# A four-layer graph network on one core: messages weighted by ScalarE, one-hots in halves, and a test by in-degree

## The chip, the cores and the metric

The kernel runs on one core of a Trainium2 chip. The metric is device time in microseconds (us). A profile of one execution gives, for each engine, when each instruction ran; the profiled execution has a time of its own, which stands beside the median of the runs below. Engine names are those of the profile: PE (TensorE), DVE (VectorE), ACT (ScalarE), POOL (GpSimd) and SP (SyncE, which here only starts DMAs).

## What is computed

The reference carries 3125 nodes with 256 features through four layers. Each layer adds a graph network and a token mixer to x, and then a mixture of experts. All four graph networks use the same 50,000 edges, drawn and sorted by destination like this:

```python
src = jax.random.randint(jax.random.fold_in(_gk, 2), (50000,), 0, 3125, jnp.int32)
dst = jnp.minimum((3125 * jax.random.uniform(jax.random.fold_in(_gk, 3), (50000,)) ** 2.0).astype(jnp.int32), 49999)
```

Layer 1's graph network (with two convolutions, each with an edge weight `ew`) and layer 3's (three convolutions, without weights) are, cut to what matters:

```python
def _hconv(x, src, dst, ew, w1, b1, w2, b2, g, b):            # layer 1, twice
    h = jax.nn.relu(x @ w1 + b1)
    msg = ew[:, None] * h[src]
    agg = jax.ops.segment_sum(msg, dst, num_segments=x.shape[0])
    h = agg @ w2 + b2
    return jax.nn.relu(_bn(h, g, b))

deg = jnp.zeros((n,), x.dtype).at[dst].add(1.0) + 1.0         # layer 3
dinv = jax.lax.rsqrt(deg)
h = jnp.tanh(gcn_conv(x, W1, b1, src, dst, dinv))             # 256 -> 512
h = jnp.tanh(gcn_conv(h, W2, b2, src, dst, dinv))             # 512 -> 512
out = gcn_conv(h, W3, b3, src, dst, dinv)                     # 512 -> 256
```

where `gcn_conv` is A·(h W) + b, with the adjacency A (self loops included) scaled by `dinv` on both sides.

## The kernel before

Nodes lie in NB = 25 blocks of P = 128. The edges of each block are padded to whole slots of 128; there are room and instructions for NS = 416 slots, which are handled in groups of G = 4, so a loop over the edges has 104 groups. Line numbers are those of the kernel before, as in its profile.

**A loop over the edges** is `gather_sum` (L550). For each group it issues four indirect DMAs from POOL (`gather`, L531), each of which fetches the source rows of one slot into the tile `msg`; it makes four one-hot matrices on DVE from the slot's local destinations `dl` (with weights: four `tensor_scalar` at L566, which compare with the column numbers `cols` and multiply by `ew`; without: one `tensor_tensor` over 128x512 in `one_hot`, L538); it adds the group before it into `agg` (L544, four adds on DVE, each at an address that L527 loads into a register); it lets PE multiply one-hots by messages (L585, called from `sum_group`), with four PSUM tiles named `g`; and it takes one step of the other work that was passed in as `steps`. The messages have `ahead` tiles of 128x1024, seven where nothing else is said. Afterwards the build orders the instructions of each engine, so neighbours on an engine need not be neighbours in the source.

**Layer 1** (L1681) has two such loops with weights, each 256 wide. In both, `both()` takes a step of the mixer `mix1` and a step of `more` per group. In the first loop `more` is `sorted_edges`, in the second it is `counts` (L2071). `counts` prepares layer 3: it writes a dense matrix of edge counts between all nodes, `counted`, to DRAM, in bfloat16. It goes over NR = 40 runs of edges. Per run it makes two one-hots of 128x3200 in bfloat16 on DVE (`ohs` and `ohd`, L2085, one buffer each); `on`, an identity or zero (L2089, ACT); for 25 blocks a 128x128 matmul (L2098) on top of `on` times the previous run's tile (L2096); copies of the sums into the tile `T` (L2100, ACT); an identity added to the own block of `T` where a run begins (L2108, DVE); two ACT passes over `T` (L2111) that write to `junk` and accumulate whatever lies over FULL = 255.5 into `over`; and the DMA of `T` to `counted` (L2112, SP). It yields twice per run, so 80 times, once per group in the first 80 of 104 groups.

At its end (L2114 to L2120) `over` is reduced to a column of `unfit`, which holds for three conditions whether a partition violates them; the columns are summed over partitions into one number, `gathers`.

**Layer 3** (L2325) reads that number into a register and takes one of two branches, both of which are in the program:

```python
with tc.If(unfit > 0, preferred_fallthrough_block=False) as cmp:
    with self.pool("xT", 1) as xp:
        self.xT = xp.tile([P, 2, NP], F32, name="xT")
        self.gcn3()
    self.routes(begin, route)
with cmp.Else():
    self.dense3(begin, route)
```

`dense3` (L2123) multiplies by `counted`: 100 products (four sets of 25 blocks), each a DMA of 800 KB into a tile `a` and 75 matmuls (L2154) with activations split into three bfloat16 parts; the scaling by `di` = 1/sqrt(deg + 1) is at L2160, the weight matmuls are at L465 and L2214, and the mixer's steps and `routes` (the assignment of tokens to experts, which ends with 50 indirect DMAs `sent<-xs` on POOL at L1402) run beside the products. `gcn3` (L2256) does the same with three unweighted loops over the edges, `gather_sum` with `ahead=6`: it normalizes x and stores a table of 256-wide rows; the first loop gathers from it, with the mixer's steps beside it; each of 25 blocks is scaled, transposed, multiplied by W1 and passed through tanh, and stored as a 512-wide row table; the second loop gathers 512-wide; groups of four blocks go through W2, tanh and W3 into a third table, 256 wide; the third loop gathers from it; the sum is scaled and added to x. Then come `routes`, with nothing beside them. The experts (`rest`) follow either branch.

`self.deg`, from which both branches take `di`, is made in layer 0: an extra column of the messages is set to one (L854), summed like the features, and copied out at L901. So it is the number of edges that end at each node.

Of the kernel before, what the change touches and what calls it, by code (L numbers as in the profile page):

```python
# [9 lines left out]
F32 = mybir.dt.float32  # L10
BF16 = mybir.dt.bfloat16
I32 = mybir.dt.int32
AF = mybir.ActivationFunctionType
# [6 lines left out]
P = 128  # L20
# [10 lines left out]
G = 4  # L31
# [33 lines left out]
class Net:  # L65
# [466 lines left out]
            out=out, out_offset=None, in_=table,  # L532
            in_offset=bass.IndirectOffsetOnAxis(ap=self.src[:, t:t + 1], axis=0))

    def one_hot(self, pool, g):

        oh = pool.tile([P, G, P], F32, name="oh")
        self.nc.vector.tensor_tensor(oh, bc(self.dl[:, g * G:(g + 1) * G], [None, None, P]),  # L538
                                     bc(self.cols, [None, G, None]), ALU.is_equal)
        return oh  # L540

    def add_to(self, agg, t, q, w):
# [4 lines left out]
        for j in range(G):  # L547
            self.add_to(agg, g * G + j, q[j], agg.shape[2])

    def gather_sum(self, pool, ps, table, w, agg, weighted=False, ahead=7, steps=None):  # L550

        nc = self.nc
        sums = {}
        n = 1024 // w
        for g in range(NS // G):
            msg = []
            for j in range(G):
                if j % n == 0:
                    m = pool.tile([P, n, w], F32, name="msg", bufs=ahead)
                self.gather(m[:, j % n, :], table, g * G + j)  # L560
                msg.append(m[:, j % n, :])
            if weighted:
                oh = pool.tile([P, G, P], F32, name="oh", bufs=3)
                for j in range(G):
                    t = g * G + j
                    nc.vector.tensor_scalar(oh[:, j, :], self.cols, self.dl[:, t:t + 1], self.ew[:, t:t + 1],  # L566
                                            op0=ALU.is_equal, op1=ALU.mult)
# [1113 lines left out]
    def layer1(self):  # L1681
        nc, tc = self.nc, self.tc
        self.norm_x()
        with self.pool("rooms", 1) as c, self.pool("gnn", 1) as gw, self.pool("gnn2", 2) as gp, \
                self.pool("mix", 1) as mw, self.pool("mix2", 2) as mp, \
                self.pool("ps1", 3, PSUM) as ps, ExitStack() as own:
            pool = Pools(gw, gp, CONV_ONE)

            sums = ps.tile([P, 3, P], F32, name="acc0", bufs=1)
            nc.scalar.copy(sums[:, 1, :], self.cols)  # L1690
            nc.vector.tensor_scalar(sums[:, 2, :], self.cols, 1.0, None, op0=ALU.add)
            steps = self.mix1(mw, mp, ps, sums[:, 0, :])

            def loop(tab, agg, more):
                def both():
                    for _ in range(NS // G):
                        next(steps, None)
                        next(more, None)
                        yield

                self.gather_sum(pool, ps, tab, D, agg, weighted=True, steps=both())
                for _ in more:
                    pass


            self.rooms = c.tile([P, NR, 2 * NB], BF16, name="rooms")
            self.run_blk = c.tile([1, NR], I32, name="run_blk")
            self.goes_on, self.begins = (c.tile([P, NR], F32, name=n) for n in ("goes_on", "begins"))

            self.unfit = c.tile([P, 3], F32, name="unfit")  # L1710

            tab, agg, *rest = self.conv_head(pool, ps, 1, self.xT)
            with self.pool("sort", 1, side="right") as bp:
                with ExitStack() as inner:
                    loop(tab, agg, self.sorted_edges(bp, ps, inner, sums[:, 1, :]))
            with self.pool("res", 1, side="right") as hp:
                hT = hp.tile([P, 2, NP], F32, name="hT")
                self.conv_tail(pool, ps, agg, *rest, hT)
                sc, sh = self.batch_norm(pool, hT, self.plain(gw, "L1_gnn_bn1_g"), self.plain(gw, "L1_gnn_bn1_b"), "bn")
                self.relu_of(hT, sc, sh)  # L1720
                tab, agg, *rest = self.conv_head(pool, ps, 2, hT)
            with self.pool("count", 1, side="right") as bp:
                loop(tab, agg, self.counts(bp, ps, sums[:, 1:, :]))
            hp = own.enter_context(self.pool("res", 1, side="right"))
            hT = hp.tile([P, 2, NP], F32, name="hT")
# [345 lines left out]
    def counts(self, p, ps, cols):  # L2071
# [1 line left out]
        nc = self.nc  # L2073
        ident = p.tile([P, P], BF16, name="identb")
        nc.vector.tensor_copy(ident, self.ident)
        full = p.tile([P, 1], F32, name="full")
        nc.vector.memset(full, -FULL)
        over = p.tile([P, NR, 2], F32, name="over")
        nc.vector.memset(over, 0.0)
        last = None  # L2080
        for u in range(NR):
            oh = []
            for k, name in enumerate(("ohs", "ohd")):
                t = p.tile([P, NB, P], BF16, name=name)
                nc.vector.tensor_tensor(t, bc(self.rooms[:, u, k * NB:(k + 1) * NB], [None, None, P]),  # L2085
                                        bc(cols[:, 1 - k, :], [None, NB, None]), ALU.is_equal)
                oh.append(t)
            on = p.tile([P, P], BF16, name="on", bufs=2)
            nc.scalar.mul(on, ident, self.goes_on[:, u:u + 1])  # L2089
            yield  # L2090
            T = p.tile([P, NB, P], BF16, name="T", bufs=2)
            for k0 in range(0, NB, 4):
                n = min(4, NB - k0)
                q = ps.tile([P, 512], F32, name="mm")[:, :n * P]
                if last is not None:
                    nc.tensor.matmul(q, on, last[:, k0:k0 + n, :], start=True, stop=False)  # L2096
                for k in range(n):
                    nc.tensor.matmul(q[:, k * P:(k + 1) * P], oh[0][:, k0 + k, :], oh[1][:, k0 + k, :],  # L2098
                                     start=last is None, stop=last is None or k == n - 1)
                nc.scalar.copy(T[:, k0:k0 + n, :], q.rearrange("p (k d) -> p k d", d=P))  # L2100
                if k0 == 12:
                    yield

            Tf = T.rearrange("p k d -> p (k d)")
            r = nc.values_load(self.run_blk[0:1, u:u + 1], engines=(ET.DVE, ET.SP), min_val=0, max_val=NB - 1,
                               skip_runtime_bounds_check_because=IN_RANGE)
            own = Tf[:, bass.ds(r * P, P)]
            nc.vector.scalar_tensor_tensor(own, ident, self.begins[:, u:u + 1], own, op0=ALU.mult, op1=ALU.add)  # L2108
            for i, k0, k1 in ((0, 0, 13), (1, 13, NB)):
                junk = p.tile([P, 13 * P], BF16, name="junk")[:, :(k1 - k0) * P]  # L2110
                nc.scalar.activation(junk, Tf[:, k0 * P:k1 * P], AF.Relu, bias=full, accum_out=over[:, u, i:i + 1])  # L2111
            nc.sync.dma_start(self.counted[bass.ds(r * P, P), :], Tf)  # L2112
            last = T
        nc.vector.tensor_reduce(self.unfit[:, 1:2], over.rearrange("p u i -> p (u i)"), axis=AX.X, op=ALU.max)  # L2114
        nc.vector.tensor_scalar(self.unfit[:, 1:2], self.unfit[:, 1:2], 0.0, None, op0=ALU.is_gt)
        one = p.tile([P, 1], F32, name="one")
        nc.vector.tensor_reduce(one, self.unfit, axis=AX.X, op=ALU.add)
        q = ps.tile([P, 512], F32, name="mm")
# [328 lines left out]
```

## Time and profile before

| | us |
|---|---|
| median of three runs | 6186.31 (6184.32 to 6188.53) |
| the profiled execution | 6189.69 |
| its span | 6187.9 (mean granted TensorE clock 0.862) |
| layer 1's first loop, first to last gather | 1500 to 2058 |
| layer 1's second loop, first gather to last add | 2166.1 to 2836.0 |
| layer 3's branch, `di` to the last `sent<-xs` | 4476.8 to 5696.8 |

Over the span PE is busy 75%, DVE 53%, POOL 39% and ACT 25%. These are averages over stages with different limits, so the stages are read one by one: windows of the trace give each engine's busy time and instructions ("x") in a stretch, with the granted clock, the DMA share and GB/s; tables by line give busy time, the mean duration of one instruction in ns, and what ended the idle time before it.

### The profile page before, as it was taken

What the parts mean: (1) busy time and instruction counts of PE and PEld (TensorE: products, weight loads), DVE (VectorE), ACT (ScalarE), POOL (GpSimd) and SP (SyncE); (2) the same over time, 40 slices, a digit from 0 to 9 for tenths busy, and PEclk for the clock granted to TensorE, in tenths of its full rate; (3) what the DMA queues carried; (4) which work ended last, traced back from release to release, by engine and by line L of the source; (5) the groups of instructions that cost most, each with busy time, mean ns of one, the idle gap of its engine ahead of it and who ended that gap; (6) DMA issues with size and microseconds to landing.
All of it is one profiled execution on the core that took longest, in us unless ns stands there. A gap on an engine that the chain in (4) does not pass through costs nothing.

```text
span 6187.9 us, 81932 instructions
## 1 busy us (share of the span) xinstructions
PE 4643.9 (75%) x25310; PEld 3283.6 (53%) x25310; DVE 3297.2 (53%) x8633; ACT 1567.8 (25%) x4108; POOL 2397.0 (39%) x2340
## 2 busy tenths in 40 slices
PE   1848775696778766656697758880699999997997
PEld 1314343583565344443683235550456888786996
DVE  6448777426798388876326567776142100134222
ACT  1213233222100245432222123311144201111332
POOL 1537774322777275552423567771100000011111
PEclk9969887797897777777798879995899999998998
DMA  2744442553333144332564324430111322124554
GB/s 82 220 122 117 118 120 66 179 177 102 93 97 102 55 151 137 130 117 66 160 184 131 99 72 123 120 116 27 57 62 65 131 99 73 59 96 153 182 172 160
DMA packets 385095, 710.60 MB, mean 115 GB/s; under 512 B 100817, under 2 KB 223256, under 8 KB 384652
## 3 DMA queue, kind: packets, MB, share of 16 engines
q1 hardware_dynamic: 266431, 425.79, 21.6%
q0 software_dynamic: 108064, 269.63, 14.9%
q10 hardware_dynamic: 10157, 9.80, 0.5%
q8 instruction: 213, 3.49, 0.2%
q14 instruction: 230, 1.88, 0.1%
HBM read 571.51 MB, written 133.47 MB: 114 GB/s over the span
## 4 chain that ended last, share of the span: by engine, by line
PE 43%; issue 17%; DVE 15%; POOL 11%; DMA 8%; ACT 3%; DVEq 2%; SPq 1%; ACTq 0%; another core or an unknown queue 0%; POOLq 0%
PE dn L2154 13%; PE mm L465 6%; POOL msg L531 6%; PE g L585 4%; PE g L862 3%; DMA msg<-L_gnn_htab,src 2%; PE h L1507 2%; PE y L1520 2%; DVE ohd L2085 2%; POOL ase L531 2%; DVE agg L544 2%; DMA terms<-outr 2%; POOL back L1524 1%; PE mm L2214 1%; PE mm L2098 1%
## 5 line engine op out<-in xcount | busy, mean ns | idle before, releaser
L531 POOL DMA_INDIRECT msg<-L_gnn_c_tab,src x832 | 827.4, 995 | 606.6 <-issue 225.3
L531 POOL DMA_INDIRECT msg<-L_gnn_htab,src x832 | 887.5, 1067 | 383.5 <-issue 213.0
L544 DVE TENSOR_TENSOR agg<-agg,g 128x256 f32 (+2 forms) x1664 | 697.6, 419 | 215.0 <-PE g L862 96.3
L2154 PEld LDWEIGHTS <-a 128*128 128x128 bf16 x7500 | 736.2, 98 | 116.9 <-issue 28.3
L862 PE MATMUL g<-msg,oh 128*128 128x261 f32 (+1 forms) x1664 | 568.7, 450 | 194.0 <-DVE agg L544 176.5
L1402 POOL DMA_INDIRECT sent<-xs,ids x150 | 153.0, 1020 | 1292.9 <-DMA yb<-done,backs 1036.3
L585 PE MATMUL g<-msg,oh 128*128 128x256 f32 x1664 | 581.6, 484 | 86.5 <-DMA msg<-L_gnn_c_tab,src 35.5
L862 PEld LDWEIGHTS g<-msg,oh 128*128 128x128 f32 x1664 | 314.2, 211 | 433.6 <-DVE agg L544 328.2
L585 PEld LDWEIGHTS g<-msg,oh 128*128 128x128 f32 x1664 | 358.5, 238 | 235.4 <-DVE oh L566 86.8
L1524 POOL DMA_INDIRECT back<-y,toi x168 | 163.6, 974 | 787.1 <-DVE y L1523 510.6
L1507 PE MATMUL h<-xe,w 128*128 128x128 f32 x3584 | 436.8, 278 | 5.3 <-DMA w<-in_L_ffn_W 5.2
L2154 PE MATMUL dn<-ha,a 128*128 128x256 bf16 x3750 | 428.5, 275 | 7.7 <-ACT ha L2139 6.5
L1520 PE MATMUL y<-w,hT 128*128 x1792 | 431.2, 388 | 0.0
L1511 ACT ACTIVATE hT<-h,br 128x128 f32<-128x128 f32 x896 | 256.4, 369 | 669.5 <-issue 573.4
L1507 PEld LDWEIGHTS h<-xe,w 128*128 128x128 f32 x3584 | 422.0, 195 | 7.0 <-DVE toi L1496 6.2
L2154 PE MATMUL dn<-hb,a 128*128 128x256 bf16 x3750 | 418.2, 273 | 0.0
L1520 PEld LDWEIGHTS y<-w,hT 128*128 128x128 f32 x1792 | 326.5, 190 | 57.0
L1523 DVE COPY y<-y 128x256 f32<-128x256 f32 x168 | 71.2, 424 | 521.7 <-PE y L1520 521.5
L851 DVE TENSOR_TENSOR msg<-msg,alpha 128x1024 f32<-128x1024 f32 x208 | 254.1, 1222 | 133.4 <-DMA msg<-L_gnn_htab,src 119.9
L819 ACT COPY stage<-dm 128x24 bf16 (+1 forms) x832 | 182.5, 220 | 452.1 <-PE pd L825 281.6
L531 POOL DMA_INDIRECT ase<-tab,src x208 | 231.8, 1115 | 148.4 <-PE q L657 85.3
L566 DVE TENSOR_SCALAR oh<-cols,dl,ew 128x128 f32<-128x128 f32 x832 | 266.6, 350 | 0.0
(730 smaller groups left out, 7155.0 us busy)
## 6 DMA issues: line engine op xcount, KB each, us to landing
a<-counted SPq DMA_DIRECT2D x100, 800.0 KB
w<-in_L_ffn_W SPq DMA_DIRECT2D x128, 512.0 KB
w<-in_L_ffn_W SPq DMA_DIRECT2D x64, 1024.0 KB
counted<-T SPq DMA_DIRECT2D x40, 800.0 KB
dr<-dl_rows SPq DMA_DIRECT2D x104, 256.0 KB
sent<-zeros SPq DMA_DIRECT2D x25, 1040.0 KB
xr<-sent SPq DMA_DIRECT2D x168, 130.0 KB
lw<-lo_rows SPq DMA_DIRECT2D x78, 256.0 KB
```

The source lines that it names most:

```text
L465: nc.tensor.matmul(q, xT[:, k, t * P:(t + 1) * P], w[:, k, cols], start=(k == 0 and bias is None), stop=(k == nk - 1))
L531: self.nc.gpsimd.indirect_dma_start(out=out, out_offset=None, in_=table, in_offset=bass.IndirectOffsetOnAxis(ap=self.src[:, t:t + 1], axis=0))
L544: self.nc.vector.tensor_tensor(at, at, q, ALU.add)
L566: nc.vector.tensor_scalar(oh[:, j, :], self.cols, self.dl[:, t:t + 1], self.ew[:, t:t + 1], op0=ALU.is_equal, op1=ALU.mult)
L585: self.nc.tensor.matmul(r, oh[:, j, :], msg[j], start=True, stop=True)
L851: nc.vector.tensor_tensor(mh, mh, bc(al_, [None, None, None, C]), ALU.mult)
L862: nc.tensor.matmul(q, oh[:, j, :], msg[:, j, :], start=True, stop=True)
L1507: nc.tensor.matmul(q[:, i, :], d["w1"][:, k, c * P:(c + 1) * P], d["xe"][:, k, :], start=(k == 0), stop=(k == 1))
L1511: nc.scalar.activation(hT[:, c, :], q[:, i, :], act, bias=d["br"][:, c:c + 1])
L1520: nc.tensor.matmul(q, d["hT"][:, c, :], w2f[:, bass.ds(e * (nh * D) + c * D, D)], start=False, stop=(c == nh - 1))
L1524: s = nc.gpsimd.indirect_dma_start(out=self.back, out_offset=bass.IndirectOffsetOnAxis(ap=d["to"][:, 0:1], axis=0), in_=y, in_offset=None)
L2154: nc.tensor.matmul(q, a[:, k, :], h[:, k, i, :], start=(k == 0 and i == 0), stop=(k == NB - 1 and i == 2))
```

## The change

It has four parts, the first three in layer 1's second loop. The messages are multiplied by the edge weight on ACT, in place, and the four one-hots become one `tensor_tensor` without weights, whose column numbers are read from PSUM. A run's one-hots are made in two parts, of 12 and 13 blocks, each double-buffered, and what followed a run's sums (own block, DMA) is done by `finish` after the next run's first one-hots. The 80 yields are spread over 98 groups. And the two ACT passes over `T` are gone; the second column of `unfit` is now whether the largest `deg` of a partition is at least 255.5. Layer 1's first loop passes no `cols` and keeps its form.

```diff
-    def one_hot(self, pool, g):
+    def one_hot(self, pool, g, cols=None, **more):
-        oh = pool.tile([P, G, P], F32, name="oh")
+        oh = pool.tile([P, G, P], F32, name="oh", **more)
         self.nc.vector.tensor_tensor(oh, bc(self.dl[:, g * G:(g + 1) * G], [None, None, P]),
-                                     bc(self.cols, [None, G, None]), ALU.is_equal)
+                                     bc(self.cols if cols is None else cols, [None, G, None]), ALU.is_equal)
...
-            if weighted:
+            if weighted and cols is not None:
+                for j in range(G):
+                    nc.scalar.mul(msg[j], msg[j], self.ew[:, g * G + j:g * G + j + 1])
+                oh = self.one_hot(pool, g, cols, bufs=3)
+            elif weighted:
...
-            def loop(tab, agg, more):
+            def loop(tab, agg, more, over=80, **how):
                 def both():
-                    for _ in range(NS // G):
+                    for g in range(NS // G):
                         next(steps, None)
-                        next(more, None)
+                        for _ in range((g + 1) * 80 // over - g * 80 // over):
+                            next(more, None)
                         yield
...
-                loop(tab, agg, self.counts(bp, ps, sums[:, 1:, :]))
+                loop(tab, agg, self.counts(bp, ps, sums[:, 1:, :]), over=98, cols=sums[:, 1, :])
...
+        def finish(u, T):
             Tf = T.rearrange("p k d -> p (k d)")
             r = nc.values_load(self.run_blk[0:1, u:u + 1], engines=(ET.DVE, ET.SP), min_val=0, max_val=NB - 1,
                                skip_runtime_bounds_check_because=IN_RANGE)
             own = Tf[:, bass.ds(r * P, P)]
             nc.vector.scalar_tensor_tensor(own, ident, self.begins[:, u:u + 1], own, op0=ALU.mult, op1=ALU.add)
-            for i, k0, k1 in ((0, 0, 13), (1, 13, NB)):
-                junk = p.tile([P, 13 * P], BF16, name="junk")[:, :(k1 - k0) * P]
-                nc.scalar.activation(junk, Tf[:, k0 * P:k1 * P], AF.Relu, bias=full, accum_out=over[:, u, i:i + 1])
             nc.sync.dma_start(self.counted[bass.ds(r * P, P), :], Tf)
+        for u in range(NR):
+            T = p.tile([P, NB, P], BF16, name="T", bufs=2)
+            on = p.tile([P, P], BF16, name="on", bufs=2)
+            nc.scalar.mul(on, ident, self.goes_on[:, u:u + 1])
+            for h0, h1 in ((0, H), (H, NB)):
+                oh = []
+                for k, name in enumerate(("ohs", "ohd")):
+                    t = p.tile([P, NB - H, P], BF16, name=name, bufs=2)[:, :h1 - h0]
+                    nc.vector.tensor_tensor(t, bc(self.rooms[:, u, k * NB + h0:k * NB + h1], [None, None, P]),
+                                            bc(cols[:, 1 - k, :], [None, h1 - h0, None]), ALU.is_equal)
+                    oh.append(t)
+                if last is not None and h0 == 0:
+                    finish(u - 1, last)
+                for k0 in range(h0, h1, 4):
...
+                yield
             last = T
-        nc.vector.tensor_reduce(self.unfit[:, 1:2], over.rearrange("p u i -> p (u i)"), axis=AX.X, op=ALU.max)
-        nc.vector.tensor_scalar(self.unfit[:, 1:2], self.unfit[:, 1:2], 0.0, None, op0=ALU.is_gt)
+        finish(NR - 1, last)
+        most = p.tile([P, 1], F32, name="most")
+        nc.vector.tensor_reduce(most, self.deg, axis=AX.X, op=ALU.max)
+        nc.vector.tensor_scalar(self.unfit[:, 1:2], most, FULL, None, op0=ALU.is_ge)
         one = p.tile([P, 1], F32, name="one")
         nc.vector.tensor_reduce(one, self.unfit, axis=AX.X, op=ALU.add)
```

The lines left out of the last loop are the matmuls and copies of before, which index the half's one-hots.

More of the change, by code (lines that the diff above doesn't have):

```diff
@@ L548, in add_group, with gather_sum @@
             self.add_to(agg, g * G + j, q[j], agg.shape[2])
-    def gather_sum(self, pool, ps, table, w, agg, weighted=False, ahead=7, steps=None):
+    def gather_sum(self, pool, ps, table, w, agg, weighted=False, ahead=7, steps=None, cols=None):
         nc = self.nc
@@ L1692, in layer1 @@
             steps = self.mix1(mw, mp, ps, sums[:, 0, :])
-            def loop(tab, agg, more):
+            def loop(tab, agg, more, over=80, **how):
                 def both():
-                    for _ in range(NS // G):
+                    for g in range(NS // G):
                         next(steps, None)
-                        next(more, None)
+                        for _ in range((g + 1) * 80 // over - g * 80 // over):
+                            next(more, None)
                         yield
-                self.gather_sum(pool, ps, tab, D, agg, weighted=True, steps=both())
+                self.gather_sum(pool, ps, tab, D, agg, weighted=True, steps=both(), **how)
                 for _ in more:
@@ L2075, in counts @@
         nc.vector.tensor_copy(ident, self.ident)
[L2076 to L2079, printed above, removed]
         last = None
[L2081 to L2102, printed above, removed]
+        H = 12
+        def finish(u, T):
             Tf = T.rearrange("p k d -> p (k d)")
@@ L2108, in counts @@
             nc.vector.scalar_tensor_tensor(own, ident, self.begins[:, u:u + 1], own, op0=ALU.mult, op1=ALU.add)
-            for i, k0, k1 in ((0, 0, 13), (1, 13, NB)):
-                junk = p.tile([P, 13 * P], BF16, name="junk")[:, :(k1 - k0) * P]
-                nc.scalar.activation(junk, Tf[:, k0 * P:k1 * P], AF.Relu, bias=full, accum_out=over[:, u, i:i + 1])
             nc.sync.dma_start(self.counted[bass.ds(r * P, P), :], Tf)
+        for u in range(NR):
[12 more added lines that the diff above has]
+                for k0 in range(h0, h1, 4):
+                    n = min(4, h1 - k0)
+                    q = ps.tile([P, 512], F32, name="mm")[:, :n * P]
+                    if last is not None:
+                        nc.tensor.matmul(q, on, last[:, k0:k0 + n, :], start=True, stop=False)
+                    for k in range(n):
+                        nc.tensor.matmul(q[:, k * P:(k + 1) * P], oh[0][:, k0 - h0 + k, :], oh[1][:, k0 - h0 + k, :],
+                                         start=last is None, stop=last is None or k == n - 1)
+                    nc.scalar.copy(T[:, k0:k0 + n, :], q.rearrange("p (k d) -> p k d", d=P))
+                yield
             last = T
-        nc.vector.tensor_reduce(self.unfit[:, 1:2], over.rearrange("p u i -> p (u i)"), axis=AX.X, op=ALU.max)
-        nc.vector.tensor_scalar(self.unfit[:, 1:2], self.unfit[:, 1:2], 0.0, None, op0=ALU.is_gt)
+        finish(NR - 1, last)
+        most = p.tile([P, 1], F32, name="most")
+        nc.vector.tensor_reduce(most, self.deg, axis=AX.X, op=ALU.max)
+        nc.vector.tensor_scalar(self.unfit[:, 1:2], most, FULL, None, op0=ALU.is_ge)
         one = p.tile([P, 1], F32, name="one")
```

## The prediction

> **What bounds the kernel now.** First the windows of stages (columns: stretch, its length, busy us of PE, PEld, DVE, ACT and POOL with instructions, granted clock, DMA share, GB/s):
>
> ```profile
> 1600.00:1700.00 100.00, 71.19 (x499) 56.22 (x499) 86.36 (x176) 11.25 (x45) 78.83 (x70) 0.97 0.31 92
> 2220.00:2320.00 100.00, 65.11 (x360) 47.93 (x358) 85.81 (x142) 51.82 (x87) 69.28 (x73) 0.75 0.48 154
> 2750.00:2830.00 80.00, 59.07 (x171) 34.05 (x172) 58.59 (x180) 0.17 (x2) 60.49 (x65) 0.81 0.36 107
> 4600.00:4700.00 100.00, 100.00 (x596) 64.59 (x594) 31.52 (x71) 47.31 (x93) 0.00 (x0) 1.00 0.18 62
> ```
>
> The second row is layer 1's second loop: DVE is busy 86%, the rest of its time is waiting. The last row is layer 3: PE is never idle, at full clock, and POOL does nothing. So these two stages, which the change touches, have different limits. Now the loop by line (busy, mean ns | idle before, releasers), and one of its waits (us in total, times, longest):
>
> ```profile
> L531 POOL DMA_INDIRECT msg<-L_gnn_c_tab,src x416 | 395.4, 951 | 377.7 <-issue 111.6 <-DMA L_gnn_c_tab<-hb 107.6 <-PE g L585 83.4
> L544 DVE TENSOR_TENSOR agg<-agg,g 128x256 f32 x416 | 173.6, 417 | 41.7 <-PE g L585 26.8 <-DVE agg L544 1.8 <-PE mm L2098 1.3
> L2085 DVE TENSOR_TENSOR ohd<-rooms,acc 128x3200 bf16<-128x3200 bf16 x40 | 139.2, 3480 | 0.0
> L566 DVE TENSOR_SCALAR oh<-cols,dl,ew 128x128 f32<-128x128 f32 x404 | 127.7, 347 | 0.0
> L2111 ACT ACTIVATE junk<-T,full 128x1664 bf16<-128x1664 bf16 x40 | 67.3, 1682 | 80.4 <-DVE T L2108 79.1
> ```
> ```profile
> DVE ohs L2085 <- PE mm L2098: 49.5, 28, 3.2
> ```
>
> The reader is to see that a gather costs 0.95 us and 0.30 of issue, so 416 of them fill 521 us of POOL, whatever else happens; and that DVE's one-hots wait for PE to release their single buffer. The loop takes 670 us (2166.1 to 2836.0).
>
> **Which branch runs.** The tables by line show `dn L2154` (x7500 in two sets) and no 512-wide gather, so `gathers` was 0. Count multiplicities and in-degrees in the reference's own draw (seed 0): the most parallel edges between two nodes are 4, so the old test against 255.5 could not fire. But a destination is floor(3125·u²): node 0 gets a share of sqrt(1/3125) = 0.0179 of 50,000 edges, about 894 (drawn: 856), and nodes 1, 2 and 3 have 391, 300 and 271. `deg` is this in-degree, without normalization (a column of ones, summed). The new column of `unfit` is therefore 1 in four partitions, `gathers` is 4, and layer 3 takes `gcn3`. This bound is safe and much too coarse: it bounds a count by a row's sum. It decides the sum below.
>
> **The second loop, part by part.** Per group DVE loses four `tensor_scalar` (1.03 start to start in the loop's last stretch, 2746 to 2836) and gains one 128x512 compare:
>
> ```profile
> L538 DVE TENSOR_TENSOR oh<-dl,cols x208: 650/684/755, 150.1 to 4175.5; 128x512 f32<-128x512 f32 x104
> ```
>
> The four adds stay: 1.95 alone, 1.3 where they alternate with other work (a pair of one-hot and add takes 0.59 between runs, 0.26 of it the one-hot). Per run the one-hots cost 2 x 3.41 start to start, own 0.26, two more starts some 0.1: 7.2, over 98 groups with 40 runs 2.94 per group. Together 0.65 + 1.3 to 1.95 + 2.94 = 4.9 to 5.5 us per group, against POOL's 4 x 1.252 = 5.01. Before, the stretch 2202 to 2556 took 13.65 per two groups, 6.83 each: 6.82 of large one-hots, 0.26, eight pairs of 0.59 and 1.78 idle. The idle goes with the second buffer; what is late next is POOL. ACT loses 2 passes (1.68 + 1.57 + 2 x 0.19 per run) and gains 4 scalings of 128x256 a group: between 474 ns (L2160) and 588 ns (L922), 1.9 to 2.35 us; with its copies (158.5 us over 98 groups, 1.6) 3.5 to 4.0, so it lies beside POOL. A scaling waits for its gather to land (some 1.8 us after POOL's instruction), and behind it on ACT stand the copies of `T`, for which own on DVE and the next run's L2096 on PE wait: up to 0.3 us per group, I estimate, since seven groups of messages are kept. PE had 4.45 busy per group at clock 0.75, under 5.3. SP starts the same 40 DMAs, one run later; nothing reads `counted` before 4484. Value: 98 x 5.3 + 6 x 5.01 + 4.3 (last gather to last add, as now) + 2 = 556, a gain of about 115. Bounds: POOL alone 521 + 11 = 532 (138), and 98 x 5.85 (5.54 and that wait) + 36 = 609 (some 60).
>
> **Layer 3's branch.** What goes: 4476.8 to 5696.8, 1220 us. What comes, priced by rows of the same operations:
>
> ```profile
> L465 PE MATMUL mm<-L_gnn_W,zT 128*128 128x512 f32 x100 | 49.6, 618 | 0.0
> L2214 PE MATMUL mm<-zT,L_gnn_W 128*128 128x512 f32 x96 | 45.1, 592 | 0.0
> L2214 PE MATMUL mm<-zb,L_gnn_W 128*128 128x512 f32 x96 | 45.1, 592 | 0.0
> L465 PE MATMUL mm<-L_gnn_W,h2T 128*128 128x256 f32 x200 | 44.3, 379 | 0.0
> ```
>
> - Norm and first table: in `dense3` the last transposes of the normalized x are at 4515; with the store 40 (36 to 45).
> - First loop, 256 wide, mixer beside it: 416 x 1.252 = 521, or 558 as layer 1's first loop took beside its mixer; with landing and last adds (3) 524 to 561, I take 540.
> - 25 blocks through W1: PE 49.6 + 50 transposes (9.6; L456 28.8 for 150) = 59; each block waits for transpose, copy, matmul, tanh and scale in only two PSUM tiles, so 3.05 a block, with the table's landing 80 (67 to 89).
> - Second loop, 512 wide: never seen with 128 rows, but the nearest row has 104 rows of 2 KB, and costs the same as one of 1 KB:
>
> ```profile
> L268 POOL DMA_INDIRECT got<-listed,chunk x4 | 4.1, 1028 | 26.2 <-DVE b L260 25.3 <-issue 0.9
> ```
>
>   DVE has 0.65 + 4 adds of twice the width (0.68, as L538 for 512) = 3.4 to 3.7, PE 8 passes of 0.43 = 3.4 at full clock, 5.2 at 0.66: both near or under 5.0. The transfers, 256 KB per 1.25 us, are 205 GB/s; the profile page's busiest slice moved 220. So 524 to 561, taken 540.
> - W2 and W3: 90.2 + 44.3 + 100 transposes (19) = 154 of PE, plus bubbles and the store: 170 (158 to 204, the latter 32 us for each of 6.25 groups of blocks if nothing overlaps).
> - Third loop, nothing beside it: 530 (524 to 561).
> - Adds to x and `routes` alone: layer 1's took 90 from the complete x (2905.9) to the last `sent<-xs` (2995.9), 24 before the first, 50 x 1.28 after; 95 (87 to 105). In `dense3` most of it was covered by PE's products; that cover is gone.
>
> Sum 1995 (1920 to 2126): +775 (+700 to +906). On engines this moves the stage from PE to POOL, whose 3 x 416 gathers are 1563 alone, more than the whole branch of before. The weight loads, the mixer's steps (2.2 us of PE each: `dense3` takes 17.16 per product of 8.29, with four steps) and the loops' one-hots lie beside POOL. With the loop's own 2.7 the first loop has 4.9 of PE per group at full clock; where a lower clock makes this 6, POOL covers it no more and it takes 624, some 80 more.
>
> Against the profiled run: 6189.7 + 775 - 115 = 6850; the median lies 3.4 lower, so **6846**.
>
> A rule that speaks against the 540: the Trainium skill, "DMA: Bandwidth & Descriptors", section Bandwidth (Measured), gives 0.95 us for a software-queue transfer of 64 KB and 6.15 for 1 MB. Interpolated, 256 KB is an estimated 2.0 us by that page, over the 1.25 pitch; if transfers did not overlap, the second loop would be about 830 and the forecast 7140. The 2 KB rows of L268, four gathers at the usual duration, are too few to refute it.
>
> **The rivals.**
> 1. The other side: `gathers` stays 0 and `dense3` runs. Place: the comparison at the end of `counts`; it decides from a largest in-degree of 255.5 upwards. For: nothing in the trace shows an in-degree. Against: the draw, where node 0 alone has over three times that, for any seed. Time: 6186 - 115 = 6071 (6048 to 6126). Chance 0.03; 0.01 more that the time ends within the bound.
> 2. The second loop gains nothing, because ACT's scalings wait in order for gathers and hold up the copies, and so the ring from PE to DVE. For: windows show DVE idle already by such rings. Against: ACT has room, messages come early. 6186 + 775 = 6961. Chance 0.10.
> 3. 512-wide rows double the instruction or saturate the queues: at the profile's mean rate of 115 GB/s a gather takes 2.28, the loop 948, time 7250; any case from 7035 up 0.08.
> 4. The loop of `gcn3` beside the mixer is bound by PE at a low clock (0.75 in the loop above): +80 with the rest as forecast, 6930, in the range. Chance 0.08.
>
> **How the numbers follow.** The forecast has 0.70. Its ends: 6186 + 700 - 138 = 6748 and 6186 + 906 - 60 = 7032, so I give 6745 to 7035, which holds cases 2 and 4 as well, about 0.85. Within 0.2%, some 12 us, is no change for a measurement of this kernel: faster 0.03, same 0.01, slower 0.96.
>
> **What would show it.** In the profile after: no rows of L2154's products, 1248 instead of no gathers from layer 3's tables, POOL busy some 52% of the span (2397 + 1248 x 0.95 of 6850) instead of 39%; gathers per group near 5.3 in the second loop, junk rows gone, and layer 1's `ohs` no longer idle for PE; 512-wide gathers near 1 us; the experts starting some 660 later. I would be wrong if `dn` rows are still there (then 6071), or if the second loop is not shorter than 609.

## The result

The changed kernel takes 6999.86 us in the median (6996.54 to 7002.76, four runs), the kernel before 6187.07 beside it: 1.1314 times, 95% interval 1.1295 to 1.1334. The forecast was 6846 with 6745 to 7035, slower. The sign, the branch and the range are right; of the two large terms one, the loop, is wrong by 137 us.

**Windows of the profile after** (same columns as before: stretch, its length, busy us of PE, PEld, DVE, ACT and POOL, granted clock, DMA share, GB/s). The first two are the changed loop, the others the three gather loops of layer 3:

```profile
2220.00:2320.00 100.00, 65.10 (x318) 43.99 (x318) 73.47 (x104) 53.43 (x116) 61.39 (x65) 0.79 0.42 135
2750.00:2830.00 80.00, 46.34 (x235) 32.60 (x235) 58.02 (x81) 38.60 (x84) 40.12 (x43) 0.72 0.35 117
...
4540.00:5080.00 540.00, 435.60 (x1199) 224.38 (x1199) 279.62 (x629) 34.93 (x82) 411.85 (x416) 0.82 0.35 102
...
5170.00:5690.00 520.00, 427.03 (x793) 122.84 (x791) 330.17 (x493) 0.00 (x0) 399.67 (x396) 0.99 0.69 200
...
5880.00:6400.00 520.00, 443.95 (x821) 195.10 (x822) 232.73 (x510) 0.00 (x0) 394.83 (x412) 0.58 0.36 104
```

In layer 3 POOL has taken PE's place: in the mean it issues a gather every 1.26 to 1.32 us through all three loops. In layer 1's loop DVE fell from 86% to 73%, but POOL fell too, from 73 gathers per 100 us to 65. Work was taken off the engine that bound the loop, and the loop did not get faster. Now no engine is full there, which is the mark of a ring of waits: each engine stands still until the next one in the circle has done its part.

**Where the time went**, by first and last instructions in the two traces:

| stage | before | after | difference | forecast |
|---|---|---|---|---|
| layer 1's second loop, first gather to last add | 2166.1 to 2836.0, 670 | 2168.8 to 2860.7, 692 | +22 | -115 |
| `di` of layer 3 starts at | 4476.8 | 4502.8 | +26 (the loop's 22 included) | -115 |
| layer 3's branch, `di` to the last `sent<-xs` | 1220 | 4502.8 to 6517.9, 2015 | +795 | +775 |
| from there to the end of the span | 491 | 481 | -10 | 0 |

26 + 795 - 10 = 811, the difference of the spans (6998.6 - 6187.9).

Of the loop's +22, 21 lie behind its last gather: from the first gather to the last it takes 664.6 before and 665.6 after, and from the start of the last gather to the end of the last add 5.3 and 26.3. So the gathers went no faster, 6.4 us a group in both, where the forecast had 5.3.

**The branch by line** (line, engine, operation, names, shape, count | busy us, mean ns | idle before). First the 512-wide loop, then the third loop's gathers, then W1 and W2:

```profile
L590 PE MATMUL g<-msg,oh 128*128 128x512 f32 x832 | 450.3, 635 | 104.8 <-DMA msg<-L_tab,src 76.6 <-DVE agg L544 20.9
L531 POOL DMA_INDIRECT msg<-L_tab,src x416 | 420.7, 1011 | 212.8 <-DMA L_tab<-agg 86.4 <-issue 64.3 <-DMA msg<-L_tab,src 38.1
L544 DVE TENSOR_TENSOR agg<-agg,g 128x512 f32 x416 | 285.0, 685 | 30.1 <-PE g L590 10.6 <-DVE agg L544 1.5 <-DVE oh L538 0.4
```
```profile
L531 POOL DMA_INDIRECT msg<-L_tab,src x416 | 399.0, 959 | 293.3 <-DMA L_tab<-agg 166.9 <-issue 120.9 <-PE g L590 5.2
```
```profile
L465 PE MATMUL mm<-L_gnn_W,zT 128*128 128x512 f32 x100 | 51.4, 637 | 0.0
```
```profile
L2317 PE MATMUL mm<-agg,L_gnn_W 128*128 128x512 f32 x192 | 85.9, 606 | 0.0
```

A gather of 128 rows of 2 KB costs POOL 1011 ns, one of 1 KB 959. The 512-wide adds cost 685 ns, as the forecast took from a compare of that width.

**The changed loop by line** (the stretch 2163 to 2840, behind which the last six groups of adds lie), **and its waits** (the stretch 2163 to 2862; us in total, times, longest):

```profile
L531 POOL DMA_INDIRECT msg<-L_gnn_c_tab,src x416 | 393.3, 945 | 380.3 <-issue 205.7 <-PE mm L2114 111.0 <-ACT msg L565 44.0
...
L565 ACT ACTIVATE msg<-msg,ew 128x256 f32<-128x256 f32 x416 | 207.2, 509 | 306.9 <-DMA msg<-L_gnn_c_tab,src 298.8 <-PE g L590 6.7
...
L544 DVE TENSOR_TENSOR agg<-agg,g 128x256 f32 x392 | 163.2, 416 | 63.9 <-PE g L590 25.1 <-DVE agg L544 12.8 <-DVE oh L538 6.9
...
L2103 DVE TENSOR_TENSOR ohd<-rooms,acc 128x1664 bf16<-128x1664 bf16 x40 | 75.2, 1879 | 0.0
...
L538 DVE TENSOR_TENSOR oh<-dl,acc 128x512 f32<-128x512 f32 x98 | 66.9, 683 | 81.8 <-PE g L590 81.7
```
```profile
ACT msg L565 <- DMA msg<-L_gnn_c_tab,src: 298.8, 291, 6.3
POOL msg L531 <- issue: 205.7, 372, 7.5
PE mm L2112 <- ACT T L2116: 175.8, 57, 14.4
...
DVE oh L538 <- PE g L590: 81.7, 39, 14.2
```

Every price is as forecast: a scaling 509 ns, a one-hot 683, a half of a run's one-hots 1.75 or 1.88. What is new is the first wait: ACT spends 299 us waiting for gathers to land (before, PE's matmuls and weight loads waited 36 us for landings), and PE 176 waiting for ACT's copies. The timeline of one turn (start, us, engine, line; idle before it and its releaser), engine by engine:

```profile
2409.78 0.51 ACT L565 ACTIVATE msg<-msg,ew 128x256 f32<-128x256 f32 x1 [0.84 <-DMA msg<-L_gnn_c_tab,src]
2412.72 0.51 ACT L565 ACTIVATE msg<-msg,ew 128x256 f32<-128x256 f32 x1 [2.43 <-DMA msg<-L_gnn_c_tab,src]
2413.14 0.56 ACT L2116 CAST T<-mm 128x512 bf16<-128x512 f32 x1
```
```profile
2409.68 0.39 PE L2114 MATMUL mm<-ohd,ohs 128*128 128x128 bf16 x4
2413.75 0.59 PE L2112 MATMUL mm<-T,on 128*128 128x512 bf16 x1 [3.69 <-ACT T L2116]
```
```profile
2417.45 0.69 DVE L538 TENSOR_TENSOR oh<-dl,acc 128x512 f32<-128x512 f32 x1 [4.32 <-PE g L590]
```
```profile
2411.77 0.94 POOL L531 DMA_INDIRECT msg<-L_gnn_c_tab,src  x1 [0.30 <-issue]
2418.15 0.94 POOL L531 DMA_INDIRECT msg<-L_gnn_c_tab,src  x1 [5.44 <-issue]
```

ACT waits 2.43 for a gather; behind it stands the copy of a run's sums; PE waits 3.69 for that copy, DVE 4.32 for PE, and POOL stands still for 5.44. The profile names no releaser for POOL's wait, but a count does: up to 2418, 164 slots are gathered and 140 multiplied, there are message tiles for 28 slots, and the next gather needs the tile of slots 137 to 140, whose matmuls have just ended (2417.4). Counting starts up to 2405: 158 slots gathered, 156 scaled, but only 134 multiplied. The gathers are 24 slots, six groups, ahead of the matmuls, and the scalings 22, of the 28. (Before, at the same time, 167 were gathered and 143 multiplied: the same lag of 24, but only PE's work waited for a landing.)

### The profile page after: what moved, and what is told of

Read it like the earlier page. It is cut to its first block, busy times and chain, and to the rows that moved or that the text cites. A ratio compares the mean times of both kernels' runs of the same rounds, so it can differ in the third digit from the quotient of the medians.

```text
span 6998.6 us, 77733 instructions
## 1 busy us (share of the span) xinstructions
PE 5087.9 (73%) x20306; PEld 3073.6 (44%) x20306; DVE 3976.3 (57%) x9779; ACT 1478.4 (21%) x4099; POOL 3627.2 (52%) x3588
## 4 chain that ended last, share of the span: by engine, by line
PE 16%; issue 14%; POOL 14%; DMA 9%; DVE 6%; ACT 1%; DVEq 0%; ACTq 0%; SPq 0%; POOLq 0%
POOL msg L531 10%; DMA msg<-L_tab,src 6%; PE mm L465 3%; PE g L590 3%; POOL ase L531 2%; PE g L867 1%; PE mm L2317 1%; PE h L1512 1%; PE y L1525 1%; POOL back L1529 1%; DMA msg<-L_gnn_htab,src 1%; PE mm L456 1%; DVE agg L544 1%; PE y L465 1%; PE h L502 1%
## 5 line engine op out<-in xcount | busy, mean ns | idle before, releaser
L590 PE MATMUL g<-msg,oh 128*128 128x256 f32 (+1 forms) x4160 | 1813.0, 554 | 392.6 <-DMA msg<-L_tab,src 232.3
L544 DVE TENSOR_TENSOR agg<-agg,g 128x256 f32 (+3 forms) x2912 | 1331.1, 457 | 569.5 <-PE g L590 326.3
L531 POOL DMA_INDIRECT msg<-L_tab,src x1248 | 1231.7, 987 | 675.1 <-issue 294.0
L590 PEld LDWEIGHTS g<-msg,oh 128*128 128x128 f32 x4160 | 857.6, 239 | 1299.8 <-DVE agg L544 535.0
L538 DVE TENSOR_TENSOR oh<-dl,cols 128x512 f32<-128x512 f32 x520 | 356.8, 686 | 427.2 <-PE g L590 422.4
L867 PEld LDWEIGHTS g<-msg,oh 128*128 128x128 f32 x1664 | 317.0, 214 | 435.6 <-DVE agg L544 331.0
L565 ACT ACTIVATE msg<-msg,ew 128x256 f32<-128x256 f32 x416 | 207.2, 509 | 306.9 <-DMA msg<-L_gnn_c_tab,src 298.8
L2112 PE MATMUL mm<-T,on 128*128 128x512 bf16 (+1 forms) x273 | 113.7, 436 | 193.2 <-ACT T L2116 175.8
```

Of the source, the lines that this page charges most:

```text
L531: self.nc.gpsimd.indirect_dma_start(out=out, out_offset=None, in_=table, in_offset=bass.IndirectOffsetOnAxis(ap=self.src[:, t:t + 1], axis=0))
L544: self.nc.vector.tensor_tensor(at, at, q, ALU.add)
L565: nc.scalar.mul(msg[j], msg[j], self.ew[:, g * G + j:g * G + j + 1])
L590: self.nc.tensor.matmul(r, oh[:, j, :], msg[j], start=True, stop=True)
L867: nc.tensor.matmul(q, oh[:, j, :], msg[:, j, :], start=True, stop=True)
```

## The experiments

They ran on three chips where the kernel before takes 6775 to 6877 us, 10 to 11% more than in the result. The excess lies in the gather loops, not in all stages: layer 3's dense branch takes 1237 to 1249 there instead of 1220, and what follows it 490 to 492 as before. The profiles show waits of theirs for which they name no releaser ("remote"). So every run is compared only with the kernel before on its own chip, and a first theory's absolute times (6187 plus or minus) are read as differences. Loop times are first gather to last add in one profile of each run; layer 1's first loop, whose code only one run touches, differs by up to 32 us between these profiles (662 to 694), so a difference of that size between two loop times says little by itself. "Dense" says that layer 3 takes the branch that the kernel before takes.

The diffs are cut to the lines that matter.

**The two halves of the change.** The loop alone, and the branch alone:

```diff
 # e1, e5, e12: the changed kernel
-        nc.vector.tensor_scalar(self.unfit[:, 1:2], most, FULL, None, op0=ALU.is_ge)
+        nc.vector.tensor_scalar(self.unfit[:, 1:2], most, 16384.0, None, op0=ALU.is_ge)
 # e2: the kernel before
-        nc.vector.tensor_reduce(self.unfit[:, 1:2], over.rearrange("p u i -> p (u i)"), axis=AX.X, op=ALU.max)
-        nc.vector.tensor_scalar(self.unfit[:, 1:2], self.unfit[:, 1:2], 0.0, None, op0=ALU.is_gt)
+        most = p.tile([P, 1], F32, name="most")
+        nc.vector.tensor_reduce(most, self.deg, axis=AX.X, op=ALU.max)
+        nc.vector.tensor_scalar(self.unfit[:, 1:2], most, FULL, None, op0=ALU.is_ge)
```

> The changed kernel, but the test asks whether an in-degree is at least 16384 instead of 255.5, so layer 3 keeps its dense branch and only layer 1's second loop differs from before. Theory A (the loop itself is longer: ScalarE's scalings wait in order for gathers, its copies of the run's sums stand behind them, and the loop from TensorE to the message buffers closes): 670 becomes 692 us and layer 1 ends 23 to 26 later, so 6187 + 25 = 6212 (6200 to 6225). Rival (the forecast: the loop is 115 shorter when the branch is taken out of the picture): 6072.

> The kernel before, with the test by in-degree at 255.5 in place of the reduction of the accumulated counts; loop, runs and the two passes over T stay. Theory A: the branch by gathers costs 797 more than the dense one (2017 against 1220 us in the two profiles) and the experts' stage after it is 12 shorter: 6187 + 785 = 6972 (6955 to 6985). Rival: the price of the branch depends on the changed loop (tables, buffers, code that lies elsewhere); then it lies outside these bounds.

The branch alone: 7758.86 against 6775.33, ratio 1.1453 (1.1399 to 1.1508). The test by itself, in the old kernel, makes it slower by as much as the whole change did, and more in us, though on another chip. It is 984 dearer, not 785: here `gcn3` with `routes` takes 2229 (5048.6 to 7277.6) instead of 2015, while `dense3` in the run with the loop alone takes 1237, close to 1220. That lies outside the bounds, as the rival said. This run alone doesn't refute its reason, a price that depends on layer 1's loop; but the excess is better laid to the chip, where gather loops stretch that nothing in the change touches (layer 1's first loop from 565 to 673) and the products don't.

The loop alone: 6748.79, ratio 0.9957 (0.9928 to 0.9985), so 27 us faster, neither 25 slower nor 115 faster. Its loop takes 729, that of before (in the run with the branch alone) 795. A change of sign between chips called for a repeat:

> The same kernel as in the run with the loop alone, since that run's chip was 9% slower in all stages, with long waits for a queue that the profile doesn't know. Theory A: on a chip like that of the first two profiles 25 us more than before (loop 692 against 670); on one like the last, 27 less, as there. Rival: the loop is shorter than before on either.

0.9918 (0.9876 to 0.9960) on the second chip, and 0.9919 (0.9885 to 0.9954) on the third (below). On the slower chips the changed loop is thus some 30 to 70 faster in the kernel's time; in the first two profiles it is 22 longer. The loop of before stretches by 125 from the first two profiles to this chip (670 to 795) and the changed one by 37 (692 to 729). In the loop, DVE has 94 us of waits without a releaser in the run with the branch alone, 36 of them before the large one-hots, and 3 in the run with the loop alone, so much of the difference may stand there; what makes these waits stays open.

**Which part of the loop's change does what.** First the weights alone and the rest alone:

```diff
 # e3: e1 with weights on DVE
-                loop(tab, agg, self.counts(bp, ps, sums[:, 1:, :]), over=98, cols=sums[:, 1, :])
+                loop(tab, agg, self.counts(bp, ps, sums[:, 1:, :]), over=98)
 # e4: the kernel before, with the change's one_hot and gather_sum
-                loop(tab, agg, self.counts(bp, ps, sums[:, 1:, :]))
+                loop(tab, agg, self.counts(bp, ps, sums[:, 1:, :]), cols=sums[:, 1, :])
```

> As the run with the loop alone (dense branch), but the weights go back into the four one-hots on VectorE; halves, the later own block, 98 groups and no passes over T stay. Theory A (the order on ScalarE, with the scalings among the copies, is what costs the gain): VectorE has four pairs of 0.59 and 2.94 us of large one-hots per group, 5.3, so the loop is near 560 and the time 6075 to 6110. Rival B (the halves and the own block behind the next one-hots close a ring of their own, whatever ScalarE does): 6187 or more.

> The kernel before, with one part of the change: messages weighted by ScalarE and one 128x512 one-hot per group; runs, passes over T, 80 groups and test as before. Theory A: with the two passes over T (3.6 us per run) still on ScalarE the ring through it is longer yet: 6230 to 6300. Rival (ScalarE has room, VectorE bounds): VectorE has 0.65 + 1.3 to 1.95 per group where it had 4 x 0.59, a loop shorter by 40 to longer by 25: 6145 to 6210.

With the weights back on DVE: 0.9830 (0.9782 to 0.9879), 116 below before, loop 660. With only the weights on ACT: 1.0106 (1.0066 to 1.0146), 59 above, loop 827. So the scalings on ACT cost 70 in the loop and 90 in the kernel's time on top of the halves (729 against 660, 6748.79 against 6659.28), and 59 in the kernel's time on top of the old loop (32 by the two loops); theory A is right in both signs (its 560 for the loop, forecast for a chip like the first, was not tried there), and the halves alone close no ring. Is it the position of the scalings?

```diff
 # e6: e1 with tiles for scaled messages, and ahead=5 in both loops of layer 1
...
                 for j in range(G):
-                    nc.scalar.mul(msg[j], msg[j], self.ew[:, g * G + j:g * G + j + 1])
+                    if j % 2 == 0:
+                        ws = pool.tile([P, 2, w], F32, name="wmsg", bufs=4)
+                    nc.scalar.mul(ws[:, j % 2, :], msg[j], self.ew[:, g * G + j:g * G + j + 1])
+                    msg[j] = ws[:, j % 2, :]
```

> As the run with the loop alone, but ScalarE writes the scaled messages to tiles of their own (four tiles of two slots, so two groups), and the gathered messages have five tiles instead of seven, in both loops of layer 1. So a scaling cannot stand more than two groups ahead of the matmul that reads it, and a message tile is free once it is scaled. Theory A (the scalings stand six groups ahead on ScalarE and close the loop over the message tiles): the second loop falls to 550 to 600 us, the time to 70 to 120 below before. Rival (scalings among ScalarE's copies cost the gain wherever they stand): as the run with the loop alone, within 15 us. The first loop with five tiles: at most 10 longer by either.

0.9876 (0.9838 to 0.9914): 94 below before, 24 below the loop alone on the same chip, loop 713 against 743. The intervals of the two ratios overlap, so the 24 is not clear of noise, and the 550 to 600 was not reached. First a wait of the loop alone on this chip (us in total, times, longest), then the profile of this run: the tile `msg` (what engines sat idle for, us and times), and the loop's first wait:

```profile
ACT msg L565 <- DMA msg<-L_gnn_c_tab,src: 238.8, 222, 6.1
```
```profile
  DMA msg<-L_gnn_c_tab,src: 9.0, 11
```
```profile
POOL msg L531 <- ACT wmsg L567: 183.8, 52, 7.1
```

The waits that the profile lays to landings are gone (9 us for 239; for 126 us of the scalings' waits it names no releaser), as the theory said, but a message tile is now released by a scaling, which stands among ACT's copies, and POOL waits 184 us for it. The theory falls in half: the distance of six groups accounts for at most some 30 us of the loop, and 54 of the 84 that separate the loop alone from the run with weights on DVE and row sums on this chip (743, 713 and 659) are still there. The likely reason is that a step of the messages' path has been put on an engine that also carries the runs' path, in one order; that is argued from these waits. The run also cut the gathered messages from seven tiles to five, and what that alone costs was not tried.

**Passes, halves and spread.** A test that costs little was needed: the copies of the sums accumulate each row over four blocks, and the test asks whether such a sum reaches 255.5. The sum bounds every count in it.

```diff
 # e7, e11: e3 with row sums, tested against FULL; e8: the kernel before with row sums for the passes
...
-                    nc.scalar.copy(T[:, k0:k0 + n, :], q.rearrange("p (k d) -> p k d", d=P))
+                    nc.scalar.activation(T[:, k0:k0 + n, :].rearrange("p k d -> p (k d)"), q, AF.Relu,
+                                         accum_out=over[:, u, k0 // 4:k0 // 4 + 1])
...
 # e9: e8 with the yields over 98 groups
...
-                        next(more, None)
+                        for _ in range((g + 1) * 80 // over - g * 80 // over):
+                            next(more, None)
...
 # e10: e7 with 80 groups
-                loop(tab, agg, self.counts(bp, ps, sums[:, 1:, :]), over=98)
+                loop(tab, agg, self.counts(bp, ps, sums[:, 1:, :]), over=80)
```

What was expected of the six runs, in the order e7 to e12:

> The halves, the later own block and 98 groups, with the weights on VectorE; in place of the two passes over T the copies of the sums accumulate over each row's four blocks, and the test asks whether such a sum reaches 255.5, which bounds every count in it. Dense branch by this test. Theory A: as the run with weights on VectorE: loop 560 to 600, 70 to 110 below before; the accumulation costs 7 x 0.19 us of ScalarE per run, beside VectorE. Rival: ScalarE's accumulation reads stand between the copies and TensorE waits for them: 40 below before or less.

> The kernel before, with the row sums in place of the two passes over T and nothing else: 80 groups, whole runs, single buffers, weights on VectorE. Theory A: in the first 26 runs VectorE is back to back but for 1.78 us per run, so no gain there; in the next 13 the own block waits 3.4 to 3.7 for ScalarE's copies, of which the passes may take up to all: 0 to 50 below before. Rival: the passes were what held the loop; then 90 or more below before, and halves and second buffers are worth nothing.

> The kernel with row sums and no passes (whole runs, single buffers, weights on VectorE), with the yields spread over 98 groups instead of 80 and nothing else. Theory: VectorE needs 2.36 + 7.1 x 40/98 = 5.26 per group and still idles 1.78 x 40/98 = 0.73 for TensorE to release the one-hots, 98 x 6.0 + 30 = 618 against 670: some 50 below before. Rival: the idle time grows as the groups come faster, so 0 to 20 below.

> Halves with second buffers, the later own block and row sums, with weights on VectorE, but 80 groups. Theory: without the idle 1.78 a run with its two groups takes 11.9 instead of 13.65, so 80 groups take 506 instead of 580, and the last 24, bound by POOL's gathers, some 100 instead of 90: 60 to 70 below before, so about half of the gain is the halves' and half the spread's. Rival: all of the gain is the halves' and the spread gives nothing: as the run with both, 110 to 130 below.

> The same kernel as the run with weights on VectorE and row sums: it should beat both kernels. On a chip like that of the first two profiles, loop 556 to 590, 80 to 115 below before (6071 to 6107); on one like the last two, 110 to 140 below before, as there.

> The loop of the change alone once more, beside the kernel above. Theory A: 70 to 85 us longer in the loop than the run above, as on the last two chips, on a quiet chip 100 to 135 longer, because there before's loop takes 670 and the changed one 692. Rival: on a quiet chip the scalings on ScalarE cost no more than on the others, 85 or less.

| run | against before on its chip | loop |
|---|---|---|
| no passes, second chip | 1.0013 (0.9982 to 1.0045) | 822 |
| no passes, 98 groups, third chip | 1.0000 (0.9963 to 1.0038) | 791 |
| halves, weights on DVE, row sums, 80 groups, third chip | 0.9798 (0.9751 to 0.9845) | 664 |
| the same, 98 groups, second chip | 0.9816 (0.9769 to 0.9863) | 659 |
| the same, 98 groups, third chip | 0.9829 (0.9794 to 0.9863) | 653 |
| the loop alone on the third chip | 0.9919 (0.9885 to 0.9954) | 726 |

In the kernel's time, row sums in place of the passes were worth nothing in the old loop, the spread was worth nothing with whole runs or with halves, and the halves with their second buffers and the later own block, taken together and without the passes, are all of the gain: the rival of the run with halves only holds, and the forecast that shared the gain is refuted. Which of these three steps does it, and whether they gain as much with the passes left in, was not tried. The spread also has a price at the loop's end: from the start of the last gather to the end of the last add the profiles with 98 groups take 22 to 31 us on these chips, those with 80 groups 16 to 21. On the third chip the changed loop is 73 longer than that with the weights on DVE (726 against 653), as on the other two (70 and 84); in the kernel's time the three differences are 44, 90 and 63, on the second and third chip with the row sums in one of the two. Windows of three runs of the third chip, the same stretch of each, in the order halves with weights on DVE, the changed loop, spread only:

```profile
2600.00:2700.00 100.00, 68.70 (x366) 49.33 (x365) 92.33 (x176) 32.14 (x108) 63.73 (x68) 0.81 0.47 147
```
```profile
2600.00:2700.00 100.00, 68.29 (x322) 46.69 (x323) 77.89 (x113) 50.60 (x110) 58.80 (x62) 0.76 0.42 131
```
```profile
2600.00:2700.00 100.00, 55.47 (x282) 39.37 (x280) 73.04 (x132) 23.80 (x79) 50.08 (x53) 0.71 0.37 119
```

With halves and the weights on DVE, DVE is 92% busy and POOL gathers 68 times; the changed loop has less DVE work and fewer gathers (62); whole runs with single buffers have 53, and DVE idle by 27%.

The kernel with halves, row sums and weights on DVE beats both kernels: 0.9816 and 0.9829 of before, where the change is at 1.1314. On a chip like that of the first two profiles it wasn't run, nor was any other experiment: there the loss by the scalings is argued from the trace.

## Why the prediction was right, and where it was wrong

**The branch: right.** `gathers` became positive by the in-degree of four nodes, layer 3 took `gcn3`, and no row of `dense3`'s products is left. The run with the branch alone shows that this test by itself makes the loss. By its parts, forecast and measured in the profile after:

| part | forecast | measured |
|---|---|---|
| norm and first table | 40 | 4502.8 to 4539.8, 37 |
| first loop, mixer beside it | 540 | to 5083.7, 544 |
| W1 and its table | 80 | to 5164.7, 81 |
| 512-wide loop | 540 | to 5718.6, 554 |
| W2, W3 and table | 170 | to 5878.7, 160 |
| third loop | 530 | to 6408.3, 530 |
| adds and `routes` | 95 | to 6517.9, 110 |

Seven terms, most of them priced by the nearest row of the trace, gave 1995 for 2015; none is off by more than 15. The row of four gathers of 2 KB was the right one to go by: 1011 ns with 128 rows. The table of the Trainium skill that was weighed against it ("DMA: Bandwidth & Descriptors", Bandwidth) gives, interpolated, an estimated 2.0 us for 256 KB, and so for a gather if transfers did not overlap. In the trace one goes out every 1.3 us at 200 GB/s, and a matmul that waited for its gather started 3.8 us (median) after the gather's instruction did; so transfers overlap here, and the row decides. Neither rival of the branch came: the 512-wide loop took 554 and not 948, and the loop beside the mixer took 544, with a granted clock of 0.82.

**The loop: wrong.** The step that failed is ACT's load of "3.5 to 4.0, so it lies beside POOL", with a wait of "up to 0.3 us per group, I estimate, since seven groups of messages are kept". The loop takes 6.4 us a group up to its last gather where the forecast had 5.3, and then 25 from the end of the last gather to the last add, where it took 4.3. The prediction's own sign of being wrong, a second loop not shorter than 609, came true at 692. ACT's busy time was priced right and its order was left out: an engine with room can still be the link on which others wait. The seven tiles were counted as slack, but the lag of the matmuls behind the gathers uses six of them. Rival 2 named this mechanism, at 6961 and a chance of 0.10; the measured 7000 lies 39 above it, about the loop's further 22 and the branch's 20. The argument brought against this rival, that messages come early, is what the trace refutes: ACT waits 299 us for them. But the runs don't show that the scalings make the whole miss of 137: on the other chips they cost 70 to 84 of the loop, and what they cost on the first was not measured. The range held although the loop lay outside its own bounds (a gain of 60 to 138), because the branch stayed 111 below its upper bound; that the range takes in rival 2 was said in advance, so the range speaks for the branch alone.

**The halves: mechanism right.** The 1.78 us per run that DVE waited for PE before its large one-hots do go with the second buffer (49.5 us before; in the changed loop no such wait is left), and with the weights on DVE that engine is 92% busy (third chip, 2600 to 2700). But the forecast took its 5.3 us per group partly from the spread, and the spread alone moves nothing in the kernel's time. That the weights on ACT buy DVE little could have been read from its own numbers: one compare and four adds, 1.95 to 2.6, for four pairs of 0.59.

## What to carry to other kernels

When a test picks between two code paths, work out on the real inputs what the new test says before pricing anything else: a safe bound that is too coarse costs the whole difference of the paths, here 795 us for a test that takes 0.17. When a step is moved to an engine with spare time, ask what stands behind it in that engine's order and what it waits for; if the moved step waits for a transfer and the next instruction feeds a different chain, the two chains are tied together, and buffers counted as slack may already be used up by the lag. And a cheap valid bound can lie in an instruction that is there anyway: the accumulator of a copy gave one, in place of the two passes, without any change of the time (1.0013, 0.9982 to 1.0045).

## What the runs showed of the hardware

An indirect gather of 128 rows costs POOL nearly the same for 2 KB rows as for 1 KB (1011 against 959 ns). In the third gather loop of layer 3 the granted clock was 0.58 while PE's share of busy time was 85% (444 of 520 us), and at 5.09 us per group the loop still went at POOL's pace, so the lower clock cost next to nothing there.

The chips of the experiments were slower in gather loops above all: layer 1's first loop, which no run but that with five message tiles touches, took 563 and 565 in the first two profiles and 662 to 694 on the others, while the dense branch took 1220 and 1237 to 1249. One wait of the run with the spread only, as an example of those that the first two profiles lack:

```profile
DVE agg L544 <- remote: 241.1, 58, 36.7
```

Here the profile finds no releaser. What makes these waits wasn't settled.
